# Second batch of a fused attention and expert kernel: another order of its query pairs, and pair 8-9 by seven half-size products

## Chip, core and metric

The kernel runs on one core of one Trainium2 chip. The metric is the device time of one execution in microseconds (us), as the median of several runs. One further execution is recorded by the hardware profiler; every row in this text is from that one.

## What is computed

The input `x` has 2 batches of 2048 rows of 512 numbers, all in 32-bit floats. The reference, cut to what matters here:

```python
xn = layernorm(x)
# attention on layernorm(xn) * gamma + beta
q, k, v = split(x_norm @ qkv, 3)
scores = (q @ k.T) / sqrt(512)                 # causal: row s sees keys 0..s
out = softmax(scores) @ v @ o_proj + xn
# experts on xn: 8 experts, the two best of each row, 512 -> 352 -> 512, silu
g = silu(weighted_sum_of_two_experts(xn))
result = x + out * g
```

## The kernel before

**Stages.** The kernel first normalises all rows and makes, for each block of 512 rows, keys, queries and values in DRAM (`kt_d`, `qt_d`, `v_d`; the score's scale and the two weight products are folded in beforehand). It then routes rows to experts and runs the experts. The last stage, from about 550 us on, is the attention. Only this last stage is touched by the change.

**Tiles and pairs.** The attention works on 32 query tiles of 128 rows, 16 for each batch. Because of the causal mask, tile t of a batch (0 to 15) sees t + 1 groups of 128 keys. The list `seq` (lines 1014 and 1015) says which tile stands at which position s from 0 to 31; two neighbours (even s, then s + 1) are a pair of neighbouring tiles and share one load of queries (`fetch_q`). The first batch stands at positions 0 to 15 in falling order, the second at 16 to 31. In this text a pair of the second batch is named by its two tiles, such as 8-9. Keys and values are held in blocks of 512; the second batch's four blocks are K, K+1, K+2, K+3 with `K = NBB` = 4.

**The step loop (line 1760).** All instructions are recorded in the order in which the program writes them, and every engine runs its own in that order; there is no scheduler. Step s writes the scores of the tile at position s, and the values (softmax weights times values) of an earlier one, so that the work between the two hides what other engines do. For an ordinary tile:

- `chunk_scores` (L1302): 4 TensorE (PE) matmuls for each block of up to 512 keys, into a PSUM bank; VectorE (DVE) masks the last 128 columns (L1312) and takes the row maximum (L1295). `end_scores` (L1393) joins the maxima to `nm` (L1395).
- `exponentials` (L1478): ScalarE (ACT) takes the exponentials (L1485), GpSimd (POOL) splits each 512 of them into upper and lower halves (L1495, tile `pu`), and a transposing DMA issued by SP turns each (L1501, `puT`). At the next step DVE joins the halves again (`join_p`, L1515 to 1517) into `turned`, named `pT` in the rows. Tiles with at most three key groups (`by_te`, L1504) are instead turned by PE.
- `values` (L1522): one 128x512 matmul for each group of 128 keys (L1535), at step s + 2.

**By seven products.** For pairs in `SCORED` (L1271, numbers are s // 2) the two query tiles and the two blocks of 512 keys are taken as a 2 by 2 block matrix product, and seven half-size products are made instead of eight (Strassen's scheme). `fast_scores` (L1342) writes the 7 products, each of two 128x512 matmuls (L1359), at the pair's even step, and DVE adds them up (L1365). It needs sums of query parts (`query_sums`, L1320, 4 DVE operations at the end of the step before) and sums of key parts (`block_sums`, L1331, tile `tk`, once for each batch). Blocks past the second, and so the masked one, still go through `chunk_scores`, at each tile's own step.

For pairs in `FAST` (L1272) the values are made by seven products too. `combine_p` (L1559) makes four sums of both tiles' softmax weights on DVE (L1577; s1 first, then the difference that overwrites part of the second tile, then s2 and s4); `combine_v` (L1548, L1557, tile `vT`) makes the sums of value blocks. With s the even position of the pair, the order is:

- step s + 2, after that step's own scores: DVE joins the second tile's weights, then `combine_p`; PE does `values_first` (L1604, from the first tile's raw weights, "p12") and `values_next` (L1615, "p57", whose first matmul reads s1);
- step s + 3, after that step's own scores: `values_end` (L1622, "p64", "p03").

At even and odd steps DVE also weights the gathered expert rows (L1689), between two ACT operations (L1688, L1691), and scales the output rows (`attended`, L1696 on ACT, then L1699 on DVE); L1699 is written ahead of the step's scores and joins.

**What is loaded and summed when.** `parts_b` (L1740) gives the step from which each key or value block of the second batch is loaded; keys of block K from step 12, its values from step 14. `later` (L1747) gives the steps at whose end `block_sums` and `combine_v` of the second batch are written, one DVE operation each.

Of the kernel before, what the change touches and what calls it, by code (L numbers as in the profile page):

```python
# [26 lines left out]
def gated_attention_moe(  # L27
# [33 lines left out]
    BT = 4  # L61
    TB = BT * P
    NB = NT // BT
    NBB = S // TB
# [947 lines left out]

    assert B == 2 and NBB == 4
    seq = [t for t in reversed(range(NBB * BT))]
    seq += [NBB * BT + t for t in (8, 9, 0, 1, 6, 7, 2, 3, 4, 5, 10, 11, 12, 13, 14, 15)]
    assert all(seq[s] // 2 == seq[s + 1] // 2 for s in range(0, NT, 2))
    fetch_k = fetch(aks, lambda: kp2, kt_d, "k2", "kT")
    fetch_v = fetch(avs, lambda: vp, v_d, "v2", "v")
# [249 lines left out]
    OUT = 4  # L1268


    SCORED = (0, 1, 2, 3, 13, 14, 15)  # L1271
    FAST = SCORED + (4,)  # L1272

    def place(s):
# [23 lines left out]
    def direct(s):  # L1298

        return range(2 if s // 2 in SCORED else 0, len(widths[s]))  # L1300

# [18 lines left out]
    def query_sums(s, engine):  # L1320

        q = qsums[s] = sq.tile([P, 4, ND // 2, P], F32, name=f"sq_{s}", tag="sq")
        (a11, a12), (a21, a22) = (
            [aqs[seq[s] // 2][:, d, ts(seq[s + i] % 2, P)] for d in kds] for i in range(2)
        )
        engine.tensor_tensor(q[:, 0], a21, a22, ALU.add)
        engine.tensor_tensor(q[:, 1], q[:, 0], a11, ALU.subtract)
        engine.tensor_tensor(q[:, 2], a11, a21, ALU.subtract)
        engine.tensor_tensor(q[:, 3], a12, q[:, 1], ALU.subtract)
# [341 lines left out]
    def gather_y(s):  # L1671

        rows[s] = [op.tile([P, 2, D], F32, name=f"yg0_{s}", tag="yg0")]
        for i in range(2):
            rows[s].append(op.tile([P, D], F32, name=f"yg1_{s + i}", tag="yg1"))
            n = seq[s + i]
            for k, y in enumerate((rows[s][0][:, i, :], rows[s][-1])):
                nc.gpsimd.indirect_dma_start(  # L1678
                    out=y, out_offset=None, in_=y_d,
                    in_offset=bass.IndirectOffsetOnAxis(ap=posi[k][:, n : n + 1], axis=0),  # L1680
                )
# [57 lines left out]
    K = NBB  # L1739
# [6 lines left out]
    later = {}  # L1746
    for steps, f, b in (  # L1747
        ((10, 10, 11, 11), combine_v, K + 2), ((12, 12, 13, 13), combine_v, K + 1),
        ((20, 21, 22, 23), block_sums, K), ((24, 25, 26, 27), combine_v, K),
    ):  # L1750
        for i, step in enumerate(steps):
            later.setdefault(step, []).append((f, b, (i + 1,)))
# [7 lines left out]
    for s in range(NT + OUT + 2):  # L1760
        fast = s // 2 - 1 in FAST
        pair = (s, s + 1) if s // 2 in SCORED else (s,)
        if s < NT and (s % 2 == 0 or len(pair) == 1):
# [30 lines left out]
        if s == NT - 1:  # L1794
            gather_y(NT - 2)
        if s % 2 and s > 3 and s // 2 + 1 in SCORED:
            query_sums(s + 1, nc.vector)
# [143 lines left out]
```

## Time and profile before

| | |
|---|---|
| median of 3 runs | 1008.23 us (1008.15 to 1008.6) |
| the profiled execution | 1007.83 us, of which its span is 1006.0 us and 1.83 us lie around it |
| DVE, ACT, POOL busy | 716.9, 403.2, 483.3 us |
| attention of the second batch by position, PE from | s = 16 at 777.3 us |
| the pair's 7 products at s = 26, 28, 30, PE | 865.75 to 877.77, 893.22 to 905.24, 932.42 to 944.44 us |
| last matmul ends | 1002.2 us |

How to read it: a row of the timeline gives its start, its length, the engine, the line, the operation, and the tiles as out<-in. The PE rows of 32-bit matmuls come as two records for each matmul of the program (x28 are 14 matmuls). "Idle before" is the time an engine stood still ahead of a row, with what ended it; PEld is the load of weights, which overlaps PE. PEclk is the clock that TensorE was granted, as a share of the full one. A chain of waits follows the program back from its last instruction.

### The profile page before, as it was taken

The numbers are of one execution on the slowest core, as the hardware profiler recorded it, in microseconds if no ns is written. First come the engines' busy times: TensorE is split into PE (matmuls) and PEld (weight loads), VectorE is DVE, ScalarE is ACT, GpSimd is POOL, SyncE is SP. The second block draws the span as 40 slices with busy tenths as digits, with TensorE's granted clock in tenths as the row PEclk, the third lists the DMA queues.
The fourth block names the chain that finished last, engine by engine and source line by source line (L and its number), as shares of the span: only waits on it lengthen the run. The fifth ranks groups of instructions, "written<-read, shape, count | busy, mean of one in ns | idle before, by whom it ended". The sixth has DMA issues, their size and how long they took to land. (4 is left out here: it accounts for less than half of the span.)

```text
span 1006.0 us, 13431 instructions
## 1 busy us (share of the span) xinstructions
PE 999.9 (99%) x3924; PEld 665.3 (66%) x3924; DVE 716.9 (71%) x1396; ACT 403.2 (40%) x804; POOL 483.3 (48%) x475
## 2 busy tenths in 40 slices
PE   9999999999999999999999999999999999999998
PEld 5888888874567767766753448677675544447577
DVE  6996746897887777677744579668576556878667
ACT  3344445322444454444445112232335535442241
POOL 4474564004644454444332165254557776764272
PEclk9999999999999999999999999999999999999999
DMA  8689996978999999999999576274677768753361
GB/s 293 193 264 293 329 286 258 349 249 240 202 227 220 211 208 221 217 200 222 216 218 242 164 193 147 78 206 104 183 199 239 225 200 240 207 141 86 92 165 42
DMA packets 296647, 207.96 MB, mean 207 GB/s; under 512 B 230776, under 2 KB 243832, under 8 KB 296576
## 3 DMA queue, kind: packets, MB, share of 16 engines
q1 hardware_dynamic: 282432, 163.56, 63.2%
q0 software_dynamic: 10400, 34.63, 12.5%
q10 hardware_dynamic: 3744, 8.91, 2.4%
q8 instruction: 34, 0.56, 0.2%
q14 instruction: 37, 0.30, 0.1%
HBM read 92.35 MB, written 60.03 MB: 151 GB/s over the span
## 5 line engine op out<-in xcount | busy, mean ns | idle before, releaser
L1195 PE MATMUL py<-arena,ht 128*128 (+3 forms) x396 | 176.7, 593 | 0.0
L1307 PE MATMUL ps<-k,q 128*128 128x512 f32 (+3 forms) x416 | 143.0, 495 | 0.3 <-PEq L1455 0.3
L1495 POOL COPY pu<-pT 128x1024 uint16<-128x1024 uint16 (+2 forms) x74 | 82.5, 1146 | 118.1 <-ACT pT L1485 59.1
L1166 POOL COPY hu<-h 128x704 uint16<-128x704 uint16 x66 | 61.9, 956 | 155.8 <-issue 121.7
L1195 PEld LDWEIGHTS py<-arena,ht 128*128 128x128 f32 (+3 forms) x396 | 71.8, 185 | 80.7 <-issue 76.9
L1307 PEld LDWEIGHTS ps<-k,q 128*128 128x128 f32 x416 | 74.7, 190 | 67.1 <-issue 56.5
L970 POOL DMA_INDIRECT xs<-zu_d,toki x66 | 77.6, 1176 | 70.2 <-DVE toki L791 55.6
L1181 ACT ACTIVATE ht<-ht,b1sel 128x128 f32<-128x128 f32 (+3 forms) x216 | 67.9, 380 | 88.1 <-DVE ht L1175 88.1
L1145 DVE TENSOR_TENSOR h<-p,h 128x176 f32<-128x176 f32 x182 | 55.5, 337 | 60.7 <-PE p L1138 57.2
L1678 POOL DMA_INDIRECT yg<-y_d,posi x64 | 67.4, 1053 | 36.9 <-DVE yg L1689 21.9
L1535 PE MATMUL po<-v,pT 128*128 128x512 f32 x152 | 67.9, 592 | 0.0
L347 POOL COPY zu<-z 128x1024 uint16<-128x1024 uint16 x32 | 39.9, 1245 | 55.7 <-DVE z L332 55.7
L1517 DVE COPY pT<-puT 128x1024 uint16<-128x1024 uint16 (+2 forms) x74 | 54.1, 759 | 8.8 <-DMA puT<-pu 8.6
L1485 ACT ACTIVATE pT<-pT,nm 128x1024 f32<-128x1024 f32 x14 | 16.1, 1148 | 110.3 <-DVE nm L1395 72.0
L1203 ACT COPY y<-py 128x512 f32<-128x512 f32 x55 | 32.2, 585 | 62.3 <-PE py L1195 48.4
L1485 ACT ACTIVATE pT<-ps,nm 128x512 f32<-128x512 f32 (+3 forms) x52 | 30.1, 581 | 62.5 <-DVE nm L1395 38.8
L1365 DVE TENSOR_TENSOR pT<-p,pT 128x512 f32<-128x512 f32 x49 | 32.9, 687 | 25.8 <-PE p L1359 22.1
L1535 PEld LDWEIGHTS po<-v,pT 128*128 128x128 f32 x152 | 28.6, 190 | 31.9 <-issue 30.1
L1707 POOL TENSOR_TENSOR o<-o,yg 128x512 f32<-128x512 f32 x30 | 42.0, 1398 | 14.3 <-DVE o L1699 14.1
L1699 DVE SCALAR_TENSOR_TENSOR o<-xo,xscale,o 128x512 f32<-128x512 f32 x30 | 25.9, 871 | 30.1 <-ACT o L1696 30.1
L1046 DVE COPY xT<-xhT 128x1024 uint16<-128x1024 uint16 x66 | 45.2, 712 | 2.3 <-DMA xhT<-xs 2.0
L1708 POOL TENSOR_TENSOR o<-o,xo 128x512 f32<-128x512 f32 x30 | 43.0, 1432 | 2.4
(342 smaller groups left out, 2142.9 us busy)
## 6 DMA issues: line engine op xcount, KB each, us to landing
y_d<-y SPq DMA_DIRECT2D x66, 256.0 KB, 4.4
zu_d<-zu SPq DMA_DIRECT2D x32, 264.0 KB, 2.8
kt_d<-kT SPq DMA_DIRECT2D x16, 512.0 KB, 5.9
q<-qt_d SPq DMA_DIRECT2D x32, 256.0 KB, 5.4
k<-kt_d SPq DMA_DIRECT2D x32, 256.0 KB, 4.7
v<-v_d SPq DMA_DIRECT2D x32, 256.0 KB, 5.6
xo<-in_x_dram SPq DMA_DIRECT2D x32, 256.0 KB, 3.8
x<-in_x_dram SPq DMA_DIRECT2D x30, 256.0 KB, 4.9
```

Of the source, the lines that this page charges most:

```text
L970: nc.gpsimd.indirect_dma_start(out=xs, out_offset=None, in_=zu_d, in_offset=bass.IndirectOffsetOnAxis(ap=toki[:, order[i] : order[i] + 1], ...
L1046: nc.vector.tensor_copy(xT.bitcast(U16).rearrange("p c (t h) -> p c t h", h=2), xhs.pop(i).rearrange("p (h c) t -> p c t h", h=2),)
L1145: nc.vector.tensor_tensor(out, x, y, ALU.add)
L1166: nc.gpsimd.tensor_copy(hu[:, :, :H], h.bitcast(U16).rearrange("p (d h) -> p h d", h=2))
L1181: nc.scalar.activation(ht[:hn, c, at], ht[:hn, c, at], AF.Silu, bias=b1sel[:hn, c, j : j + 1])
L1195: nc.tensor.matmul(py[at, :], lhsT=ht[:k, c, at], rhs=rhs[n], start=(c == 0), stop=(c == NH - 1),)
L1307: nc.tensor.matmul(ps[:, :w], lhsT=aqs[seq[s] // 2][:, c, ts(t % 2, P)], rhs=aks[first + j][:, c, :w], start=(c == 0), stop=(c == ND - 1),)
L1485: nc.scalar.activation(turned[s][:, at:end], src, AF.Exp, bias=nm, accum_out=rs[:, j : j + 1])
L1495: nc.gpsimd.tensor_copy(pu[:, : 2 * w].rearrange("p (h d) -> p h d", h=2), turned[s][:, k : k + w].bitcast(U16).rearrange("p (d h) -> p h ...
L1517: nc.vector.tensor_copy(turned[s][:, k : k + w].bitcast(U16).rearrange("p (i t h) -> p i t h", t=P, h=2), puT[:, : 2 * w // P, :].rearrang ...
L1535: nc.tensor.matmul(dst, lhsT=turned[s][:, ts(k, P)], rhs=avs[first + k // BT][:, k % BT, cols], start=(start and k == k0), stop=(k == k1 - 1),
L1678: nc.gpsimd.indirect_dma_start(out=y, out_offset=None, in_=y_d, in_offset=bass.IndirectOffsetOnAxis(ap=posi[k][:, n : n + 1], axis=0),)
```

## The change

It changes three lists. The second batch's pairs stood in the order 8-9, 0-1, 6-7, 2-3, 4-5, 10-11, 12-13, 14-15, the last three by seven products; they now stand in the order 6-7, 4-5, 8-9, 0-1, 10-11, 2-3, 12-13, 14-15, with 8-9, 10-11, 12-13 and 14-15 by seven products, scores and values both. Keys are summed at steps 15 to 18 instead of 20 to 23, values of block K at steps 18 to 21 instead of 24 to 27. Loads keep their steps.

```diff
     seq = [t for t in reversed(range(NBB * BT))]
-    seq += [NBB * BT + t for t in (8, 9, 0, 1, 6, 7, 2, 3, 4, 5, 10, 11, 12, 13, 14, 15)]
+    seq += [NBB * BT + t for t in (6, 7, 4, 5, 8, 9, 0, 1, 10, 11, 2, 3, 12, 13, 14, 15)]
...
-    SCORED = (0, 1, 2, 3, 13, 14, 15)
+    SCORED = (0, 1, 2, 3, 10, 12, 14, 15)
     FAST = SCORED + (4,)
...
         ((10, 10, 11, 11), combine_v, K + 2), ((12, 12, 13, 13), combine_v, K + 1),
-        ((20, 21, 22, 23), block_sums, K), ((24, 25, 26, 27), combine_v, K),
+        ((15, 16, 17, 18), block_sums, K), ((18, 19, 20, 21), combine_v, K),
     ):
```

## Prediction

> **What bounds the kernel now.** I read, in this order: the page's busy times, the waits of PE, the chain of waits, the timeline around a pair by seven, and the clock in short windows.
>
> ```profile
> PE 999.9 (99%) x3924; PEld 665.3 (66%) x3924; DVE 716.9 (71%) x1396; ACT 403.2 (40%) x804; POOL 483.3 (48%) x475
> ```
>
> ```profile
> engine line waited for: us in total, times, longest us
> PE warm L870 <- DVE b1s L181: 1.1, 1, 1.1
> PE p L1583 <- DVE u L1600: 0.4, 1, 0.4
> PE ps L1307 <- PEq L1455: 0.3, 1, 0.3
> PE pz L370 <- ACT zT L371: 0.3, 1, 0.3
> ```
>
> PE is the bound everywhere: it waited 2.1 us in the whole span, and in the second batch (from 777.3 us) not once. So a matmul removed is time gained, and a wait of PE added is time lost, each in full. The chain gives the prices:
>
> ```profile
> 694.16 0.89 PE ps L1307 x8
> ...
> 865.75 12.02 PE p L1359 x28
> ...
> 909.56 4.32 PE p L1583 x20
> ```
>
> A matmul has two records. One 128x512 matmul is 12.02/14 = 0.859 us, one 128x256 is 4.32/10 = 0.432 us, four of 128 columns are 0.89 us. What must be hidden behind them is seen at pair 10-11. Its second tile (11) ends its scores at 887.9 us:
>
> ```profile
> 887.91 5.31 PE L1535 MATMUL po<-v,pT 128*128 128x512 f32 x12
> 893.06 3.60 PE L1359 MATMUL p<-k,q 128*128 128x512 f32 x8
> ...
> 905.07 4.49 PE L1307 MATMUL ps<-k,q 128*128 128x512 f32 x16
> 909.40 4.48 PE L1583 MATMUL p<-v,pT 128*128 128x256 f32 x20
> ...
> 914.15 2.11 PE L1583 MATMUL p<-vT,s 128*128 128x256 f32 x9
> ```
>
> Between those scores and the first matmul that needs the tile's softmax weights (914.15, p57, which reads s1) PE has 26.2 us of other work: 5.15 of values, the next pair's seven products (12.02), 4.33 of scores, 4.75 of p12. In the meantime the others run this path:
>
> ```profile
> 891.25 1.76 DVE L1517 COPY pT<-puT 128x1024 uint16<-128x1024 uint16 x3
> 892.92 0.15 DVE L1395 TENSOR_REDUCE nm<-mx 128x1 f32<-128x2 f32 x1
> 893.17 1.15 ACT L1485 ACTIVATE pT<-pT,nm 128x1024 f32<-128x1024 f32 x1 [7.67 <-DVE ri L1659]
> 894.47 3.46 POOL L1495 COPY pu<-pT 128x1024 uint16<-128x1024 uint16 x3 [4.69 <-ACT pT L1485]
> 895.54 4.03 SPq L1501 DMA_TRANSPOSE puT<-pu  x3
> ...
> 911.17 0.83 DVE L1577 TENSOR_TENSOR s<-pT 128x640 f32<-128x640 f32 x1
> ```
>
> Two things matter. The maximum nm of tile 11 stands behind the three joins of tile 10 (L1517) on DVE. And after nm the path is long: first transpose 2.6 us later, three of them 1.35 us apart, each landing 3.4 us after its issue (the transposes' own view in this window), then joins and s1.
>
> **What the change removes.** Pair 8-9 by seven: scores of two key blocks take 7x2 matmuls of 512 columns instead of 16, so 2 x 0.859 = 1.72 us. Its values took 9 + 10 = 19 matmuls of 512 columns, 16.31 us; now they take 9 (p12) + 8 (p57) + 17 (p64, p03) = 34 of 256 columns, 14.68 us: 1.63 us. The order of instructions shows that this is really made. Together 3.35 us off PE. The other pairs' matmuls are only moved.
>
> **What it adds at no cost.** DVE gets for pair 8-9 seven additions (0.69 each), four query sums (0.41 to 1.49), four weight sums and seven half additions (0.42). DVE is busy 3.5 to 8.5 of every 10 us from 780 to 870, so this fits. The key sums move to steps 15 to 18 (1.44, 1.20, 1.97, 1.20 us on DVE) and the block-K value sums to 18 to 21 (0.7 to 1.4 each). There pairs 6-7 and 4-5 are ordinary; from a tile's scores to its values lie 13.9 us of PE (0.86 + 1.72 + 0.11 + 6.87 + 4.32 for tile 6). Keys of block K were already read at step 16, so they are there by the end of step 15. I take 0; with the cover gone, 2 us at most. A gain there is excluded, since PE does not wait now. SP: loads of block K+3 (four issues, 2.0 us) stand between the transposes of tiles 8 and 9, in a gap of 6 us: 0, at most 0.5.
>
> **What it adds on the path.** A long pair is now followed by a short one, so the 12.02 us of products that lay under the path above are gone.
>
> *Pair 8-9.* Let T be the end of its seventh product. PE then has 0.89 (tile 8's masked block), 4.29 (five key groups of tile 4), 1.73 (tile 9's block: scores end at T+6.9), 5.15 (tile 5's values), 0.89 (tile 0's scores), p12 3.89; p57 is due at T+16.8, only 9.9 us after tile 9's scores. The path: at position 26 before, nm came 3.9 us after the seventh product (877.77 to 881.66); here 3.65, as its block is narrower. First transpose 3.0 after nm (881.66 to 884.70), T+6.7; third T+9.4; landed T+12.8. Tile 8 is joined just in time for p12, but nm of tile 9 comes behind those joins at T+13.2. From nm on two paths run. By the transposes: 2.6 + 2.7 + 3.4, last join 0.42, nm 0.15, s1 0.7: 10.0 us. By DVE's order: L1699 of the step is ahead of the joins and hangs on ACT, which does the exponentials (1.95), L1688 (1.32), a table load (1.28), after DVE's L1689 the silu (1.06), then L1696 (0.78); with DVE's L1689 and L1699, the mask and maximum and three joins that is 10.6 us. I take 10.6: s1 at T+23.8, PE waits 7.0 us.
>
> *Pair 10-11.* PE after its seventh product: 2.58, 0.86, 0.22 (transposes of tile 1), 3.43 (tile 11's scores end at T+7.1), 1.72, 2.58 (tile 2's scores), p12 4.75; p12 is due at T+11.4, p57 at T+16.1, 9.1 us after tile 11's scores. Tile 10's exponentials wait for the table load behind the copy of tile 1's transpose: T+5.4. Transposes from T+7.8 to 10.5, landed by 14.0. So p12 starts late and stops between its blocks: 1.7 us. nm of tile 11 at T+14.8; to s1 11.3 us (as above, with a 512-wide block and s1 of 640 columns): T+26.1, against T+17.8: 8.3 us.
>
> Pairs 12-13 and 14-15 keep their 12 us covers. In `values_end`, s2 and s4 (1.7 us each at most) are hidden by 3.5 us of p57 and the step's scores. So 17.0 us of waits. Bounds: with the transposes' path alone, nm 1 us earlier, 12.5; with DVE's slower rows (L1689 2.75 a pair instead of 1.41, joins up to 1.6 instead of 0.68), 21.5. I stay at 17.0, nearest the rows of position 27.
>
> **The clock after a wait.** Ahead of this, no row has a wait of PE over 1.1 us, except the end. The last matmul ends at 1002.2 us, and the windows show (PEclk is the third number from the right)
>
> ```profile
> 1004.80:1005.00 0.20, 0.00 (x0) 0.00 (x0) 0.00 (x0) 0.00 (x0) 0.00 (x0) 1.00 0.00 0
> 1005.00:1005.20 0.20, 0.00 (x0) 0.00 (x0) 0.00 (x0) 0.00 (x0) 0.00 (x0) 0.78 0.00 0
> 1005.20:1005.40 0.20, 0.00 (x0) 0.00 (x0) 0.00 (x0) 0.00 (x0) 0.00 (x0) 0.50 0.00 0
> ```
>
> so 2.9 us of idling halved the clock. How it comes back no row shows. The Trainium skill, "TensorE: Matmul & The Clock Gate", section "Part 1: The HAM clock gate (the "warmup" mystery)", says that PE drops to half rate after about one idle window of 3.4 us and returns after about as long under load. This speaks against the change: both long waits would be followed by some 3.8 us at half rate, an estimate of 1.9 us lost each, 3.8 in all. By the rows alone it would be 0; a clock slow to return, 4.6. I take 3.8: the drop is in the trace.
>
> **Sum.** -3.35 + 17.0 + 3.8 = +17.4 us. Span 1006.0 becomes 1023.4, the profiled execution 1007.83 becomes 1025.3. The median stands 0.4 us above that execution, within what I can tell: 1025.
>
> **Rivals.** (a) *Faster: the cover is enough.* If s1 came within 9.9 us of the second tile's scores, only the 3.35 us would count: 1004.9. For it: PE waited nowhere before, and pair 6-7 of the first batch, with 15.4 us of cover, needed no wait for s1. Against: from nm alone the rows make 10.0 us. It decides when nm comes at the scores' end and the transposes land 1 us sooner. 4%. (b) *Shorter waits, no clock loss*: tile 9's nm is early, L1699 off the path, 12.5 us or a little more: 12.5 - 3.35 = +9.2, 1017. For it: transposes with free DMA engines; against: the place of nm in DVE's order. 25%. (c) *Longer waits*, DVE slowed by POOL beside it as at 885 to 890, and the clock late: 21.5 + 4.6 - 3.35 = +22.8, 1031. 13%. (d) *The moved sums cancel the gain only*: the waits are mostly covered and 2 to 4 us are lost elsewhere, about 1008. 3%.
>
> **How the numbers follow.** Forecast 55%: 1020 to 1029, likeliest 1025. With (b) and (c) to their bounds the range is 1016 to 1031. About 0.2% (2 us) is what a measurement of this kernel can tell from no change. Faster has (a), 0.04; same has (d), 0.03; slower 0.93.
>
> **What would show it.** Right: PE's waits have p L1583 <- DVE s L1577, twice, 6 to 9 us, near 844 and 895 us, and PEclk drops to 0.5 right behind both; L1359 has 14 more matmuls, L1535 fewer; PE's busy time outside half clock is 3 us less; first nm of tile 9 stands behind joins. Wrong: PE without waits there (a), waits for another tile than s, a clock that stays at 1.00, or waits at positions 16 to 19, where I charged nothing.

## The result, and the profile after

The changed kernel takes 1031.54 us (median of 6 runs, 1030.38 to 1038.58) against 1008.37 us (6 runs): a ratio of 1.0242 over all runs (1.0230 by the medians), with an interval of 1.0214 to 1.027. Slower was forecast, but 1025.0 us and at most 1031. Its profiled execution took 1030.38 us with a span of 1028.6 us, 22.6 us more than before.

From its page, PE's busy time, and then the waits that are new, with us in total, times, and the longest:

```profile
PE 1001.5 (97%) x3950; PEld 672.4 (65%) x3950; DVE 735.0 (71%) x1417; ACT 403.1 (39%) x802; POOL 485.7 (47%) x475
```

```profile
PE p L1583 <- DVE s L1577: 19.6, 2, 10.6
...
PE p L1583 <- DVE pT L1517: 1.0, 2, 0.6
PE p L1583 <- DVE ri L1659: 0.5, 1, 0.5
```

The two waits for s1 stand where they were forecast; around them, PE's rows (the wait is in brackets):

```profile
839.57 3.62 PE L1583 MATMUL p<-v,pT 128*128 128x256 f32 x16
843.03 0.59 PE L1535 MATMUL p<-v,pT 128*128 128x256 f32 x2
852.71 3.75 PE L1583 MATMUL p<-vT,s 128*128 128x256 f32 x8 [9.08 <-DVE s L1577]
856.25 2.54 PE L1583 MATMUL p<-vT,pT 128*128 128x256 f32 x8
...
908.96 3.97 PE L1583 MATMUL p<-vT,s 128*128 128x256 f32 x10 [10.55 <-DVE s L1577]
```

Four matmuls of 256 columns should take 1.73 us. Behind the first wait they took 3.54 us (852.71 to 856.25). The clock says why, in short windows:

```profile
847.20:847.60 0.40, 0.00 (x0) 0.00 (x0) 0.37 (x3) 0.00 (x0) 0.40 (x1) 0.64 0.86 335
847.60:848.00 0.40, 0.00 (x0) 0.00 (x0) 0.40 (x2) 0.00 (x0) 0.38 (x1) 0.50 1.10 283
...
857.20:857.60 0.40, 0.40 (x3) 0.31 (x2) 0.37 (x3) 0.00 (x0) 0.00 (x0) 0.56 0.60 143
857.60:858.00 0.40, 0.40 (x4) 0.35 (x3) 0.40 (x2) 0.00 (x0) 0.00 (x0) 1.00 0.67 210
...
912.00:912.40 0.40, 0.40 (x3) 0.29 (x2) 0.40 (x1) 0.00 (x0) 0.00 (x0) 0.80 0.00 0
```

PE works at half rate from 852.71 to about 857.55, which loses 2.4 us. At the second place it is from 908.96 to about 912.16, 1.6 us. The sum against the span of before: -3.35 (matmuls removed, as forecast) + 21.1 (waits that were not there: 19.6, 1.0, 0.5) + 4.0 (clock) = +21.75. That leaves 0.85 of the 22.6 us. Most of it lies in how the rows are counted: rows of PE that follow without a stop overlap by 0.16 us (the one at 839.57 ends at 843.19, the next begins at 843.03), and ahead of each of the five new waits this overlap is missing. As an estimate from these rows, that is 5 x 0.16 = 0.8 us.

### The profile page after: what moved, and what is told of

It reads as the page before. It is cut to its first block, busy times and chain, and to the rows that moved or that the text cites. A ratio compares the mean times of both kernels' runs of the same rounds, so it can differ in the third digit from the quotient of the medians.

```text
span 1028.6 us, 13505 instructions
## 1 busy us (share of the span) xinstructions
PE 1001.5 (97%) x3950; PEld 672.4 (65%) x3950; DVE 735.0 (71%) x1417; ACT 403.1 (39%) x802; POOL 485.7 (47%) x475
## 5 line engine op out<-in xcount | busy, mean ns | idle before, releaser
L1495 POOL COPY pu<-pT 128x1024 uint16<-128x1024 uint16 (+3 forms) x74 | 82.6, 1148 | 120.8 <-ACT pT L1485 77.8
L1307 PE MATMUL ps<-k,q 128*128 128x512 f32 (+3 forms) x384 | 129.2, 487 | 0.3 <-PEq L1455 0.3
L1307 PEld LDWEIGHTS ps<-k,q 128*128 128x128 f32 x384 | 68.7, 190 | 59.7 <-issue 49.0
L1517 DVE COPY pT<-puT 128x1024 uint16<-128x1024 uint16 (+3 forms) x74 | 59.6, 839 | 9.5 <-DMA puT<-pu 9.5
L1583 PE MATMUL p<-vT,s 128*128 128x256 f32 x180 | 45.3, 402 | 19.6 <-DVE s L1577 19.6
L1485 ACT ACTIVATE pT<-pT,nm 128x1024 f32<-128x1024 f32 x16 | 18.4, 1148 | 110.7 <-DVE nm L1395 85.0
L1365 DVE TENSOR_TENSOR pT<-p,pT 128x512 f32<-128x512 f32 x56 | 37.6, 687 | 30.6 <-PE p L1359 26.8
L1583 PEld LDWEIGHTS p<-vT,s 128*128 128x128 f32 x180 | 35.9, 203 | 26.5 <-ACT p L1611 10.9
L1535 PE MATMUL po<-v,pT 128*128 128x512 f32 x114 | 51.2, 592 | 0.0
L1707 POOL TENSOR_TENSOR o<-o,yg 128x512 f32<-128x512 f32 x30 | 42.5, 1416 | 16.4 <-DVE o L1699 16.2
L1485 ACT ACTIVATE pT<-ps,nm 128x512 f32<-128x512 f32 (+3 forms) x48 | 27.3, 571 | 58.4 <-DVE ri L1659 32.5
L1708 POOL TENSOR_TENSOR o<-o,xo 128x512 f32<-128x512 f32 x30 | 44.7, 1491 | 2.4
```

The source lines that it names most:

```text
L1307: nc.tensor.matmul(ps[:, :w], lhsT=aqs[seq[s] // 2][:, c, ts(t % 2, P)], rhs=aks[first + j][:, c, :w], start=(c == 0), stop=(c == ND - 1),)
L1495: nc.gpsimd.tensor_copy(pu[:, : 2 * w].rearrange("p (h d) -> p h d", h=2), turned[s][:, k : k + w].bitcast(U16).rearrange("p (d h) -> p h ...
L1517: nc.vector.tensor_copy(turned[s][:, k : k + w].bitcast(U16).rearrange("p (i t h) -> p i t h", t=P, h=2), puT[:, : 2 * w // P, :].rearrang ...
L1535: nc.tensor.matmul(dst, lhsT=turned[s][:, ts(k, P)], rhs=avs[first + k // BT][:, k % BT, cols], start=(start and k == k0), stop=(k == k1 - 1),
L1583: nc.tensor.matmul(dst, lhsT=a[:, k], rhs=v(k), start=(k == 0), stop=(stop and k == n - 1))
```

## Experiments

The kernel before took 1008.0 to 1008.2 us in the runs beside each group below. Each ratio is to those, over all runs.

**Which part makes the loss.** Two kernels keep the changed order. The first takes only pair 8-9 back to ordinary products:

```diff
-    SCORED = (0, 1, 2, 3, 10, 12, 14, 15)
+    SCORED = (0, 1, 2, 3, 12, 14, 15)
```

> The changed order, but 8-9 by ordinary products. Theory: the wait near 844 us (9.1 us) and its half clock (2.4 us) go, 3.35 us of matmuls come back, the wait of pair 10-11 stays at 10.6 us: 1031.5 - 11.5 + 3.35 = 1023.4. Rival (both waits have one cause in the order of the pairs alone, or what the first wait delays is only passed on): the wait of 10-11 changes by more than 2 us, and the time lies outside 1021 to 1026.

Measured: 1023.13 us (1.0151, 1.0134 to 1.0169), and one wait for s1, of 10.2 us. The loss at 8-9 is gone and that at 10-11 stays, as the sum said: the two places add up. The second keeps scores by seven everywhere and takes only the values of 8-9 and 10-11 back:

```diff
-    FAST = SCORED + (4,)
+    FAST = (0, 1, 2, 3, 4, 14, 15)
```

> The changed kernel with the same order and the same sums and scores by seven, but the values of 8-9 and 10-11 by ordinary products. Theory (only p57, which needs the sum of both tiles' weights, has lost its cover): no wait for s1, no half clock; PE saves 1.72 us of scores at 8-9 and pays 23 x 0.859 - 41 x 0.432 = 2.05 us more at 10-11: 1008.4 + 0.3 = 1008.7. Rival (the order starves PE whatever products follow; the weights come too late for ordinary products too): waits of PE for the joins of these tiles, 4 us or more in sum, 1013 or more.

Measured: 1009.37 us (1.001, 1.0002 to 1.0018; 20 runs). The waits for s1 are gone, PEclk is 1.00 in the mean, and the only new wait is one of 0.6 us for a join. Order, early sums, scores by seven at 8-9 and ordinary values at 10-11 together cost some 1.1 us (by the interval 0.2 to 1.8), of which 0.3 was expected from the count of matmuls. The other 22 us come from the values by seven, for which s1 must be there in time.

**The clock.** PE repeats the first chain of p12 in the bank of p57, where the real product later overwrites it:

```diff
         p57 = bank(s, "p57")
+        if s in (20, 24):
+            for _ in range(4):
+                chain(p57[:, LO], combos[s][1], raw(s, 0, LO))
```

> The changed kernel, and PE repeats matmuls of 256 columns into the bank of p57 before it waits for s1 (16 of them at 8-9, 20 at 10-11; the real product overwrites them). Theory (the clock halves because PE stands still, and that costs 2.4 + 1.6 us behind the two waits): the wait for s1 shows as about 2 us each, PEclk stays at 1.00, s1 itself comes as before: 1031.5 - 4.0 = 1027.5. Rival (the clock falls for another reason, or its loss is not on the path): 1031 to 1032 with PEclk at 0.5 as before. If the repeats delay others (banks, memory): above 1032.

Measured: 1027.28 us (1.021, 1.0178 to 1.0242), 4.3 us under the changed kernel by the medians; one of its four runs took 1033.3 us. The profiles say the same without that spread: from the first scores at position 16 to the start of PE's last row it takes 242.4 us, the changed kernel 246.2, which is 3.9 us. PEclk is 1.00 throughout. Its rows at pair 8-9:

```profile
853.00 1.99 PE L1583 MATMUL p<-vT,s 128*128 128x256 f32 x8 [2.06 <-DVE s L1577]
854.83 1.90 PE L1583 MATMUL p<-vT,pT 128*128 128x256 f32 x8
```

The four matmuls take 1.83 us now. s1 came no sooner; only the half rate was taken away, and with it the forecast's third term.

**Why s1 came later than forecast.** In the changed kernel, DVE and POOL at pair 8-9, between nm (839.47) and PE's start at 852.71:

```profile
839.47 0.15 DVE L1395 TENSOR_REDUCE nm<-mx 128x1 f32<-128x2 f32 x1
...
841.02 3.03 POOL L1495 COPY pu<-pT 128x1024 uint16<-128x1024 uint16 x3 [2.88 <-ACT pT L1485]
...
842.06 2.54 DVE L1689 SCALAR_TENSOR_TENSOR yg<-yg,share,yg 128x512 f32<-128x512 f32 x2 [1.59 <-ACT yg L1688]
...
844.63 1.06 ACT L1691 ACTIVATE yg<-yg 128x1024 f32<-128x1024 f32 x1 [0.69 <-DVE yg L1689]
...
847.59 3.30 DVE L1517 COPY pT<-puT 128x1024 uint16<-128x1024 uint16 x3
...
850.68 1.33 POOL L1708 TENSOR_TENSOR o<-o,xo 128x512 f32<-128x512 f32 x1
...
850.88 1.68 DVE L1577 TENSOR_TENSOR s<-pT 128x512 f32<-128x512 f32 x1
...
851.97 1.71 POOL L1707 TENSOR_TENSOR o<-o,yg 128x512 f32<-128x512 f32 x1
...
852.59 1.64 DVE L1577 TENSOR_TENSOR pT<-pT,pT 128x512 f32<-128x512 f32 x1
```

s1 took 1.68 us where 0.7 was forecast, the joins 3.30 where two of 0.68 and one of 0.42 make 1.78. s1 ends 0.55 us after POOL's L1708 (852.01), and the next sum 0.55 us after L1707 (853.68): DVE seems to stand still until POOL's operation is over. The Trainium skill, "SBUF — State Buffer", section "Who interferes with whom", has the rule: an operation of DVE with both inputs in SBUF and one of POOL that reads SBUF share a port, and the second waits until the first has ended.

By the rule s1 costs what is left of POOL's operation (1.13 us from 850.88) and then its own time, 1.13 + 0.68 = 1.81 us as an estimate, against 1.68 measured (0.68 is a sum of this size with POOL's operations left out, below); by the single row of before it costs 0.83 at any moment. The rule as given here speaks of two inputs; the joins have one, and that POOL slows them too rests on the runs alone.

To test it, POOL's two operations were left out at four positions:

```diff
-        nc.gpsimd.tensor_tensor(o, o, g, ALU.mult)
-        nc.gpsimd.tensor_tensor(o, o, xt, ALU.add)
+        if s not in (18, 19, 22, 23):
+            nc.gpsimd.tensor_tensor(o, o, g, ALU.mult)
+            nc.gpsimd.tensor_tensor(o, o, xt, ALU.add)
```

> The changed kernel without POOL's two operations on the output rows (L1707, L1708) of positions 18, 19, 22 and 23: those four tiles leave out the product with the expert rows and the sum with the input. Theory (the path was longer than forecast because joins and s1 on DVE run beside POOL: three joins 3.30 us instead of 1.8, s1 1.68 and 1.77 us instead of 0.7 and 0.83): s1 takes 0.7 to 0.85 us, the joins ahead of it about 2.4, each wait for s1 is 2 to 2.5 us shorter, and the time is 1031.5 - 4.5 = 1027. Rival (DVE is slowed by the transfers, or the path hangs on the landing of the transposes): the waits change by under 0.7 us each, 1030 or more.

Measured: 1029.79 us (1.0208, 1.0191 to 1.0225). Its rows at both places (s1 of 8-9, then of 10-11):

```profile
851.69 1.98 DVE L1517 COPY pT<-puT 128x1024 uint16<-128x1024 uint16 x3
...
853.64 0.68 DVE L1577 TENSOR_TENSOR s<-pT 128x512 f32<-128x512 f32 x1
...
854.47 3.75 PE L1583 MATMUL p<-vT,s 128*128 128x256 f32 x8 [6.74 <-DVE s L1577]
...
907.95 0.83 DVE L1577 TENSOR_TENSOR s<-pT 128x640 f32<-128x640 f32 x1
...
908.93 4.61 PE L1583 MATMUL p<-vT,s 128*128 128x256 f32 x10 [8.76 <-DVE s L1577]
```

The durations are as expected. The waits fall to 6.74 and 8.76 us, which are close to the 7.0 and 8.3 of the forecast, though L1689 still takes 2.54 us here. The gain in time was smaller, so it was run again beside the changed kernel:

> The same kernel as the one without POOL's two operations at positions 18, 19, 22 and 23, now beside the changed kernel on the same chip, because its one profile had 4.1 us of delay ahead of the attention. Theory: 4.1 us below the changed kernel (the waits for s1 measured 15.5 instead of 19.6 us). Rival (the waits only move): less than 2 us below it.

> The changed kernel once more, as the measure for the run without POOL's two operations. 1030 to 1032; waits for s1 near 844 and 898 us of 9 and 10.5 us.

Measured: 1028.35 us against 1031.67 us (ratios 1.0201, 1.0185 to 1.0216, and 1.0231, 1.0217 to 1.0245), so 3.3 us by the medians, between the two expectations; the waits were 15.3 against 19.6 us. The half rate took a part back: behind the two waits it lasted 5.0 and 5.2 us (851.58 to 856.55, 905.98 to 911.16), in the changed kernel beside it 4.5 and 3.0 (852.99 to 857.50, 909.10 to 912.11), which is 1.3 us of loss more. From the first scores at position 16 to PE's last row the two profiles differ by 2.9 us, as 4.3 - 1.3 would have it; their spans differ by 2.1, and the rest lies ahead of the second batch.

**Where the path from nm to s1 binds.** The forecast saw two causes: nm behind the joins of the first tile, and L1699 ahead of the joins of the second. Each was moved alone. First, nm ahead of the joins:

```diff
         for k, j in chunks:
             chunk_scores(k, j)
-            if s != 3 and joins:
+            if s not in (3, 21, 25) and joins:
...
+        if s in (21, 25):
+            end_scores(s)
         if s != 3:
             for f, *args in joins:
                 f(*args)
...
-        if s < NT and s != 1:
+        if s < NT and s not in (1, 21, 25):
             end_scores(s)
```

> The changed kernel, with the maximum nm of the second tile of 8-9 and of 10-11 (steps 21 and 25) ahead of the joins of the first tile on DVE. Theory (the path starts at nm, and nm stood behind those joins): nm comes 4.4 us sooner at both places, the waits for s1 fall from 9.1 and 10.6 to about 4.7 and 6.2 us, both still long enough to halve the clock: 1031.5 - 8.8 = 1022.7. Rival (the gathered rows, the table load and L1699 between nm and the joins set the time whatever nm does): the waits fall by under 2 us each, 1028 or more.

Measured: 1034.63 us (1.0261, 1.0244 to 1.0278): slower than the changed kernel by 3 us, with 22.4 us of waits for s1. Its rows at 8-9, where the seventh product ends at 827.55 us:

```profile
835.99 0.15 DVE L1395 TENSOR_REDUCE nm<-mx 128x1 f32<-128x2 f32 x1
...
838.21 3.96 DVE L1517 COPY pT<-puT 128x1024 uint16<-128x1024 uint16 x3 [2.06 <-DMA puT<-pu]
838.79 2.00 SPq L998 DMA_DIRECT2D k<-kt_d  x4
...
841.36 5.92 SPq L1501 DMA_TRANSPOSE puT<-pu  x3
...
843.10 1.40 DVE L1689 SCALAR_TENSOR_TENSOR yg<-yg,share,yg 128x512 f32<-128x512 f32 x2
...
846.29 0.75 DVE L1699 SCALAR_TENSOR_TENSOR o<-xo,xscale,o 128x512 f32<-128x512 f32 x1 [1.79 <-ACT o L1696]
```

nm came 8.4 us after the seventh product instead of 12.9, as expected, and nothing behind it kept the gain. POOL's splits (839.06 to 842.64) now run beside the first tile's joins, which take 3.96 us instead of 2.32; L1689 stands behind these joins, and L1699 comes 1 us sooner only. The second tile's joins then take 4.9 us beside POOL instead of 3.3. The transposes are issued right behind four loads of keys, take 5.92 us to issue instead of 4.04, and land 5.7 to 7.0 us after their issue instead of 4.0, yet DVE stands still for them only 0.39 us here. At 10-11, with no loads of keys ahead, the third join waits 4.06 us for its transpose; why that one came late is open. The row of L1689 shows one thing more: it takes 1.40 us once POOL's splits are over, and 2.54 beside them in the changed kernel. The rival's step is right, its number too mild.

Next, L1696 and L1699 of steps 22 and 26 behind the sums:

```diff
-        if len(pair) == 1 or s % 2:
+        if (len(pair) == 1 or s % 2) and s not in (22, 26):
             for f, *args in late:
                 f(*args)
...
             combine_p(s - 2)
+        if s in (22, 26):
+            for f, *args in late:
+                f(*args)
```

> The changed kernel, with the scaling of the output rows (L1696 on ACT, L1699 on DVE) of steps 22 and 26 written behind the sums of weights instead of ahead of the step's joins. Theory (DVE's order sets the time of s1: L1699 hangs on the silu and holds up the mask and the joins): the joins of the second tile start when the first transpose has landed (about 4.0 us behind its issue), s1 is bound by the third landing and comes 1.5 us sooner at each place: waits of 7.6 and 9.1 us, 1031.6 - 3.0 = 1028.6. Rival (the transposes and POOL beside the joins set it anyway): the waits change by under 0.7 us, 1030.5 or more.

Measured: 1031.89 us (1.0232, 1.0219 to 1.0246), no gain; waits of 20.1 us. Its joins and s1 at 8-9:

```profile
847.15 0.69 DVE L1517 COPY pT<-puT 128x1024 uint16<-128x1024 uint16 x1 [1.06 <-DMA puT<-pu]
...
850.23 2.18 DVE L1517 COPY pT<-puT 128x512 uint16<-128x512 uint16 x1 [0.77 <-DMA puT<-pu]
850.84 1.28 POOL L1707 TENSOR_TENSOR o<-o,yg 128x512 f32<-128x512 f32 x1
...
852.39 1.68 DVE L1577 TENSOR_TENSOR s<-pT 128x512 f32<-128x512 f32 x1
```

DVE now waits for each transpose; the last join takes 2.18 us beside POOL (it began 0.6 us ahead of L1707; why it waited nevertheless is open), and s1 again 1.68. The path by the transposes ends about when the path by L1699 ended. Even with POOL out of the way it would, as an estimate: 850.23 + 0.42 + 0.14 + 0.68 is 23.7 us after the seventh product, and without POOL's two operations s1 came after 23.6 us by the other path. The theory of this run fell: taking one of the two paths away gives nothing.

**A better place for 8-9.** Four kernels look for an order in which the 3.35 us, or the 1.72 us of the scores alone, are kept. Two give 8-9 the cover of 10-11 (edits against the changed kernel, cut):

```diff
-    seq += [NBB * BT + t for t in (6, 7, 4, 5, 8, 9, 0, 1, 10, 11, 2, 3, 12, 13, 14, 15)]
+    seq += [NBB * BT + t for t in (6, 7, 0, 1, 4, 5, 2, 3, 8, 9, 10, 11, 12, 13, 14, 15)]
...
-    SCORED = (0, 1, 2, 3, 10, 12, 14, 15)
+    SCORED = (0, 1, 2, 3, 12, 13, 14, 15)
```

> Order 6-7, 0-1, 4-5, 2-3, 8-9, 10-11, 12-13, 14-15: pair 8-9 by seven products as in the changed kernel, and the sums in the same early steps, but the pair behind it is by seven too. Theory (the lost cover alone makes the loss): no wait of PE for s, the clock stays at 1.00, and only the removed matmuls count: 1008.4 - 3.35 = 1005.0. Rival 1 (the early sums or the additional sums of 8-9 on DVE cost something in any order): 1007 or more, with waits of PE in positions 16 to 25. Rival 2 (the seven products themselves are dearer than counted): no waits, but 1008 or more.

and the same with 6-7, 4-5, 2-3, 0-1 ahead of 8-9:

> Order 6-7, 4-5, 2-3, 0-1, 8-9, 10-11, 12-13, 14-15, with 8-9 by seven and the early sums: the covered place of 8-9 without the short pair between ordinary long ones that made PE wait in the earlier run with 0-1 second. Theory (each pair's wait is set by the work of the pair behind it; 4-5 covers 6-7, and four short tiles in a row turn on PE): no waits of 1 us or more in positions 16 to 21, at most the 2.0 us for s1 of 8-9 seen there: 1008.0 - 3.35 + 2 = 1006.7 at most, 1004.7 without it. Rival (8-9 by seven or the early sums cost in any order): 1010 or more with waits in positions 16 to 25.

Measured: 1016.51 us (1.0084, 1.0061 to 1.0107) and 1016.55 us (1.0093, 1.0066 to 1.0121). The first one's waits in the attention:

```profile
PE po L1535 <- DVE pT L1517: 4.9, 3, 2.5
PE p L1583 <- DVE s L1577: 2.0, 1, 2.0
```

The wait for s1 of 8-9 shrinks from 9.1 to 2.0 us under the next pair's products, so the cover makes most of it; but the ordinary pairs ahead now wait for their own joins, and 1.8 us more for no shown reason. In the second the 2.0 us stay, 2.5 us come ahead of tile 3's values, whose join ends only then, and 3.7 us where the seven products of 10-11 wait for a query sum and for ACT. In each the clock fell once, behind the wait of about 2.5 us (1.7 and 1.6 us lost). Rival 1 of the first run is not excluded by either, since early sums and additions load DVE there too. Rival 2, dearer products, is not needed: over the second batch, -3.35, the waits with their missing overlaps (9.6) and the clock (1.7) make 7.9 of the 8.4 us by which the first one is longer.

Scores alone by seven, in the order of before and at its position 16 (sums of keys at steps 13 to 15, FAST without the pair):

> The kernel before, its order kept, with pair 8-9 (position 16) by seven in the scores only, and keys of block K summed at steps 13 to 15; values of 8-9 stay ordinary. Theory (seven products pay where nothing has to wait for sums of weights): 14 instead of 16 products, no wait of PE: 1008.0 - 1.72 = 1006.3. Rival (DVE's seven additions and sums make the tile's maximum late and PE waits for joins): waits of 1 us or more at positions 16 to 19, 1008 or more.

Measured: 1018.56 us (1.0107, 1.0091 to 1.0124). PE waits 2.9 us for a query sum (L1327), which stands behind two sums of keys that take 2.2 and 2.3 us on DVE, and 5.5 us ahead of tile 8's values, where the profile names no releaser. Behind both waits the clock is at half, for some 3.9 us of loss.

And with 8-9 at position 20, between short pairs, 10-11 again covered (new lines only):

```diff
+    seq += [NBB * BT + t for t in (6, 7, 2, 3, 8, 9, 0, 1, 4, 5, 10, 11, 12, 13, 14, 15)]
...
+    SCORED = (0, 1, 2, 3, 10, 13, 14, 15)
+    FAST = (0, 1, 2, 3, 4, 13, 14, 15)
```

> Order 6-7, 2-3, 8-9, 0-1, 4-5, 10-11, 12-13, 14-15: 8-9 by seven in the scores only (values ordinary), 10-11, 12-13 and 14-15 by seven as before and each with a pair by seven behind it or at the end; keys summed at steps 15 to 18, values of block K at 24 to 27 as before. Theory (seven products pay where their late sums are covered, and scores by seven need no cover of their own; the earlier run with scores only lost on sums made too late for position 16): no wait of PE over 1 us, 1008.1 - 1.72 = 1006.4. Rival (a short pair behind a long one always costs here once DVE has the seven additions too): waits of 2 us or more, 1010 or more.

Measured: 1008.77 us (1.0005, 0.9997 to 1.0013). No wait is over 0.6 us in the attention, yet the 1.72 us are not there: the rows have gaps of up to 0.6 us ahead of the values of 6, 7, 8 and 9 and in the products of 10-11, 1.0 us in sum. With the missing overlap of 0.16 us at each of these five places that is 1.8 us, an estimate, and uses the gain up. None of the tried versions beats the kernel before.

## Why the prediction was wrong

By its own steps:

- **Matmuls removed, 3.35 us: in line with what was seen.** It is a part of every sum above that closes to within 1 us. PE's busy time is 1.6 us higher in spite of it: the half rate adds 4.0 us, and the overlaps missing at five waits some 0.8.
- **Early sums at nothing: right.** No wait at positions 16 to 19, and with the values taken back the whole rest cost some 1.1 us (1009.37), 0.8 more than its count of matmuls.
- **Where PE waits: right.** p57 for s1, twice, and p12 of 10-11 between its blocks: 1.5 us against 1.7. p57 was due 17.0 and 18.6 us after the seventh product, forecast 16.8 and 17.8.
- **nm: right.** 12.9 us after the seventh product for tile 9 (forecast 13.2), 15.1 for tile 11 (forecast 14.8).
- **From nm to s1: the step that failed.** "I take 10.6" and 11.3 became 13.1 and 13.9 us, and with that the waits 9.1 and 10.6 instead of 7.0 and 8.3. The order of the path was right; DVE's operations on it were priced as if POOL stood still. At 8-9, L1689 took 2.54 instead of 1.41, the joins 3.30 instead of 1.78, s1 1.68 instead of 0.7: 3.6 us more, while the path grew by 2.5. Of L1689's 1.1 us only 0.69 held up the silu (its row at 844.63), the rest lay beside the table load; the remaining 0.7 us cannot be split. Leaving POOL's two operations out gives back 4.1 to 4.3 us of waits.
- **Why the price was wrong.** "I stay at 17.0, nearest the rows of position 27" does not fit these rows (of the kernel before):

```profile
895.72 2.75 DVE L1689 SCALAR_TENSOR_TENSOR yg<-yg,share,yg 128x512 f32<-128x512 f32 x2 [1.80 <-ACT yg L1688]
...
903.13 1.27 POOL L1707 TENSOR_TENSOR o<-o,yg 128x512 f32<-128x512 f32 x1
904.48 1.61 POOL L1708 TENSOR_TENSOR o<-o,xo 128x512 f32<-128x512 f32 x1
...
906.74 0.68 DVE L1517 COPY pT<-puT 128x1024 uint16<-128x1024 uint16 x1
```

  L1689 took 2.75 us there as well, beside POOL's splits (894.47 to 897.93), not 1.41. And joins and s1 were quick because POOL's L1707 and L1708 had ended at 906.09, ahead of the first join and under the seven products. With that cover gone the joins come sooner and meet them. So the bound of 21.5 from DVE's slower rows was the near one: 21.1 was measured.
- **The clock, 3.8 us: right in sum, in part by luck.** It was 4.0 by the windows and 3.9 to 4.3 by filling the waits, but 2.4 and 1.6 place by place, and 3.8 to 5.1 in the other runs with both waits. What decides it stands under "What was not expected". The half rate sets in during the wait, as forecast.

The sum of rival (c), 1031, was thus right, by its own mechanism for the waits. The mechanism of the forecast held; the mis-sized term is the wait, by 4.1 us. The median lies another 1.2 us above the profiled execution. Two of the first six runs, 1034.0 and 1038.6 us, are not explained.

## What to carry to other kernels

A saving of matmuls is worth its time only if the longest chain behind the moved work still fits under what PE does next; add that chain up to the last operand, not to the first. Where the chain runs on DVE, price its operations by rows that have POOL beside them, if POOL has work in the same step. Here a long wait of PE cost itself and 1.5 to 2.7 us of half clock behind it, and taking one of two nearly equal paths away gives nothing.

## What was not expected

- The clock changed only at set moments. In the changed kernel, by the windows, these are 847.31, 857.55, 901.92 and 912.16 us, and without POOL's two operations (second run) 849.72, 856.55, 900.92 and 911.16. In each profile they lie 3.41 us or whole multiples of it apart (3, 13 and 3 times; 2, 13 and 3 times), which agrees with the window of 3.4 us that the prediction used. So where a wait falls among these moments decides what follows: in the runs with both waits the clock fell 3.3 to 4.9 us after PE stopped, and under load it took 3.0 to 5.5 us to come back.
- A wait shorter than that spacing can be enough. In the first of the orders with cover PE waited 2.46 us up to 839.50, and the clock was at half from 840.23 to 843.64. Two waits of 2.04 and 2.06 us left it at 1.00.
- The four sums of weights of 8-9 took 0.68 to 0.69 us each with POOL's two operations left out. In the changed kernel the three that ran beside them took 1.64 to 1.75 us, with no idle time shown: the wait is inside the duration.
- An earlier start (nm by 4.4 us) made the kernel 3 us slower. At 8-9 the joins took longer beside POOL, at 10-11 a transpose landed late; of the 3.6 us that the second batch grew, 2.8 are longer waits and 0.8 longer half rate.
